# A graph-attention layer: the node stage's loads in another order, and one pair's gathers in other tiles

## The chip, the core and the metric

The kernel runs on one core of a Trainium2 chip. Its time is the device time of one execution in microseconds (us); the median of three runs is given, and a profile of one further execution. The core has a matrix engine (PE, with its weight loads shown apart as PEld), a vector engine (DVE), an activation engine (ACT), GpSimd (POOL) and SyncE (SP). SP computes nothing here: it issues DMAs, in the order of the program. POOL issues the indirect DMAs that gather rows by a list of indices. "SPq" in a row is an instruction of SP's queue.

## What is computed

12,500 nodes with 128 channels, 400,000 edges sorted by their target `dst`, with random sources `src`. Cut to what matters:

```python
h = relu(layernorm(x))                                   # 12500 x 128
t_src, t_dst = h @ w_src, h @ w_dst
m = t_src[src] + b_src + t_dst[dst]                      # 400000 x 128
m = m * edge_weight * radial_mlp(edge_attr_32)
m = m @ w_sep + b_sep                                    # 8 heads of 16 + 16
score = einsum(smooth_leaky_relu(m[:, :, :16]), alpha_dot)
att = segment_softmax(score, dst)
out = x + segment_sum(m[:, :, 16:] * att, dst) @ w_proj + b_proj
```

## The kernel before

**Node stage** (lines 196 to 670). The nodes lie in 98 tiles of 128, worked on in 25 groups of four. Pass 1 (the loop at line 622, `i` from 0 to 24) normalizes a group (ACT and DVE, `norm`), turns it on PE (`turn`, with the maximum with 0 on DVE at line 341), multiplies it by `w_src` (`products(i, 0)`), copies the product out of PSUM on ACT (line 356, into one of six buffers `ms0`) and stores it to the table `t_src` in DRAM by a DMA of SP's queue (line 364). Pass 2 (the loop at line 652, `i` from 0 to 27) does the second product with `w_dst`, and stores two groups at a time to `t_dst` (four buffers `ms1`). Its groups also carry jobs out of the dictionary `extra`, and the raw rows of the first five edge pairs: POOL has gathered those from `x` during pass 1 (40 indirect DMAs, line 378), and pass 2 normalizes and turns them.

A check runs beside pass 1. The sorted targets are loaded into `cur` by four DMAs (`load_targets`, 32 partitions each, line 238) and three for the borders (`load_borders`, lines 243 and 248); `sections` copies each section's first and last target to `ends` on DVE (line 254), `falls` looks for a target below the one before it (line 430), `fits` sums that up and compares single targets (`lim`, read by `load_limits`) with thresholds. The result `bad` chooses, at line 1878, between the windowed edge stage and a general one. `ends` goes to DRAM and back, spread over all partitions (`ends_store`, `ends_load`), for `spans` and `places`. `marks` writes which neighbours differ (`same`). `weights_list` is a list of 36 loads: 15 weights, 14 blocks of weights, four of edge attributes (`load_e`), then `load_d(0)`, `load_w(0)` and `load_w(1)`, whose data lie in early buffers 11, 10 and 12 (see below).

At most eight DMAs of SP's and ACT's queues are out at a time: each takes one of eight semaphores in turn, and SP waits until the DMA that had it eight issues ago has landed.

**Edge stage** (`step(k)`, line 1597, 391 pairs of 1,024 edges). Step `k` does, for pair `k`: transposes of the gathered source rows into PSUM (`sources`, line 1130; for the first five pairs a product of the raw rows, line 1126), the term of the targets (`message`, line 1142, from target rows `md` that `load_md` fetched from `t_dst` and `split_md` split in two on ACT and DVE, lines 1058 and 1060), the radial network one to three steps ahead (`mlp1`, `mlp2`, `mlp3`), scores for pair `k - 1`, and values and sums for pair `k - 12`. `gather(k + 2, f)` issues eight indirect DMAs for a pair on POOL, one for 128 edges (line 1070). POOL has nothing else to do in this stage, so it runs as far ahead as buffers allow: pairs 5 to 12 go to `early`, buffers shared with the messages; pairs from 13 (`AHEAD`) on to six tiles `gs0` and six `gs1` (`GSB` = 6) that are used in turn, so that pair 19's DMAs wait until PE has transposed pair 13. The tiles `xs` and `gu`, one each, belong to work on finished nodes, the first of which is done at pair 40.

Early buffer 10 holds the edge weights of pair 0 until `radial(0)` (line 1119) has read them; pair 10's gather waits for that, and pair 12's for `radial(1)`.

Of the kernel before, what the change touches and what calls it, by code (L numbers as in the profile page):

```python
# [11 lines left out]
F32 = mybir.dt.float32  # L12
# [43 lines left out]
def gnn_kernel(ctx: ExitStack, tc: tile.TileContext, a: dict, out: bass.AP):  # L56
# [34 lines left out]
    def done(k):  # L91

        return 2 * (k - LAG - 2) + 2
# [102 lines left out]
    with tc.tile_pool(name="node1", bufs=1) as n1, tc.tile_pool(name="node", bufs=2) as np_, \  # L196
# [65 lines left out]

        def load_limits():

            with nc.allow_non_contiguous_dma(reason="single targets"):
                u = 0
                for k, d, n in UNIT_RUNS:
                    at = dst[done(k) * SEC:done(k) * SEC + 1]
                    nc.sync.dma_start(out=lim[:, u:u + n], in_=bass.AP(at.tensor, at.offset, [[1, 1], [2 * d * SEC, n]]))
                    u += n  # L270
                nc.sync.dma_start(out=lim[:, UNITS:UNITS + 1], in_=dst[EARLY * SEC:EARLY * SEC + 1].unsqueeze(0))
                nc.sync.dma_start(out=lim[:, UNITS + 1:UNITS + 2],
                                  in_=dst[(NS - 1) * SEC:(NS - 1) * SEC + 1].unsqueeze(0))
                nc.sync.dma_start(out=lim[:, UNITS + 2:UNITS + 3], in_=dst[2 * D * SEC:2 * D * SEC + 1].unsqueeze(0))

        def weights_list():

# [335 lines left out]
        stats(*quads[3])  # L613
        stats(*quads[4])
        roots(quads[3][0], quads[4][1])
        nc.sync.dma_start(out=w_dst, in_=a["w_dst"])
        load_limits()
        load_borders()
        more = iter(weights_list())
        for _ in range(6):  # L620
            next(more)()
        for i in range(Q):
            if i + 1 < Q:
                turn(i + 1)
            if i == 0:
                scales(quads[3][0], quads[4][1])
            if i + 3 < Q:
                norm(i + 3)
            products(i, 0)
            for j in (5, 6) if i == 0 else (i + 6,):  # L630
                if j < Q:
                    stats(*quads[j])
            j = i - i % 2 + 5
            if j < Q:
                (scales if i % 2 else roots)(quads[j][0], quads[min(j + 1, Q - 1)][1])
            if 2 <= i < 6:
                load_targets(i - 2)
            if i == 8:
                sections()
            if i > 8:  # L640
                next(more)()
            if 9 <= i < 13:
                falls(i - 9)
            if i == 14:
                fits()
            if i == 15:
                ends_store()
            if i == 18:
                ends_load()
        extra = {0: lambda: marks(0), 1: lambda: marks(1), 3: lambda: marks(2), 5: lambda: marks(3),  # L650
                 7: lambda: (spans(), places()), 10: cuts, 12: direct_ids, 14: spreads}
        for i in range(2 * RQ + 8):
            if i < Q:
                products(i, 1)
            if i % 2 == 0 and 0 <= i // 2 - 4 < RQ:
                raw_turn(i // 2 - 4)
            q = i // 2 - 1
            if i % 4 == 2 and q < RQ:
                raw_roots(q, q + 2)
            if i % 4 == 3 and q < RQ:  # L660
                raw_scales(q, q + 2)
            if i % 2 == 0 and 0 <= q - 1 < RQ:
                raw_norm(q - 1)
            if i in extra:
                extra[i]()
            for load in (next(more, None), next(more, None)):
                if load:
                    load()
            if i == 2 * RQ:
                nc.scalar.activation(silu, eps[0:1, :], AF.Silu)  # L670

    chunks = [(t, min(CH, TPI - t)) for t in range(0, TPI, CH)]

# [309 lines left out]
    def windows():  # L983
# [7 lines left out]
        with tc.tile_pool(name="ps", bufs=1, space=PSUM) as pp, \  # L991
# [70 lines left out]
            def gather(k, f):  # L1062
                if k < RAW:
                    return
                gs = early[k][:, f * SEC:(f + 1) * SEC].rearrange("p (t c) -> p t c", c=C) if k < AHEAD else \
                    lp.tile([P, TS, C], F32, name=f"gs{f}", bufs=GSB)
                u = k // 16
                idx = prep[u]
                t0 = (k % 16 * 2 + f) * TS
                sent = [nc.gpsimd.indirect_dma_start(  # L1070
                    out=gs[:, t, :], out_offset=None, in_=t_src[:, :],
                    in_offset=bass.IndirectOffsetOnAxis(ap=idx[:, t0 + t:t0 + t + 1], axis=0))
                    for t in range(tiles(k, f))]
                gath[k, f] = gs, sent
# [495 lines left out]
            def has(k):  # L1570
                return 0 <= k < NP
# [25 lines left out]
            def step(k):  # L1597
# [353 lines left out]
```

## Time and profile before

| | us |
|---|---|
| median of three runs | 4060.97 (4060.41 to 4062.98) |
| the profiled execution | 4063.28 |
| its span, first to last instruction | 4061.5 |
| PE busy (95% of the span) | 3860.1 |
| DVE busy (76%) | 3104.7 |
| POOL busy (75%) | 3033.9 |
| ACT busy (46%) | 1881.2 |

A row of the page's groups gives line, engine and operation, the tiles written and read, the count, the busy time and the mean of one in ns, and the idle time of the engine just before these instructions with what ended it. In a timeline a row is the start, the duration, the instruction, and in brackets the idle time of its engine before it and what ended that. Rows of the same kind that follow each other are merged, with their count. The chain of waits that ended last breaks off after a few instructions here and shows nothing.

### The profile page before, as it was taken

What the parts mean: (1) busy time and instruction counts of PE and PEld (TensorE: products, weight loads), DVE (VectorE), ACT (ScalarE), POOL (GpSimd) and SP (SyncE); (2) the same over time, 40 slices, a digit from 0 to 9 for tenths busy, and PEclk for the clock granted to TensorE, in tenths of its full rate; (3) what the DMA queues carried; (4) which work ended last, traced back from release to release, by engine and by line L of the source; (5) the groups of instructions that cost most, each with busy time, mean ns of one, the idle gap of its engine ahead of it and who ended that gap; (6) DMA issues with size and microseconds to landing.
All of it is one profiled execution on the core that took longest, in us unless ns stands there. A gap on an engine that the chain in (4) does not pass through costs nothing. (4 is left out here: it accounts for less than half of the span.)

```text
span 4061.5 us, 84578 instructions
## 1 busy us (share of the span) xinstructions
PE 3860.1 (95%) x27826; PEld 2345.3 (58%) x27826; DVE 3104.7 (76%) x5579; ACT 1881.2 (46%) x3825; POOL 3033.9 (75%) x3193
## 2 busy tenths in 40 slices
PE   6899999999999999999999999999999999999997
PEld 6355655555655555555555555555555555555555
DVE  7577777777777777777777777777777777777876
ACT  6554444444454444444444444444444444444441
POOL 5777777777777777777777777777777777777775
PEclk8999999999999999999999999999999999999998
DMA  7777777777777777776777777777777777777772
GB/s 237 215 176 197 195 198 195 192 185 192 201 180 191 195 184 178 191 188 179 186 186 193 184 185 195 190 180 190 199 191 183 195 189 195 181 201 198 195 183 59
DMA packets 534922, 764.24 MB, mean 188 GB/s; under 512 B 123966, under 2 KB 336862, under 8 KB 534363
## 3 DMA queue, kind: packets, MB, share of 16 engines
q1 hardware_dynamic: 431003, 549.87, 46.8%
q0 software_dynamic: 101888, 207.34, 24.4%
q8 instruction: 226, 3.70, 0.4%
q14 instruction: 221, 1.81, 0.2%
q10 hardware_dynamic: 1584, 1.51, 0.1%
HBM read 633.31 MB, written 126.68 MB: 187 GB/s over the span
## 5 line engine op out<-in xcount | busy, mean ns | idle before, releaser
L1070 POOL DMA_INDIRECT gs<-t_src,idx x3021 | 2876.1, 952 | 928.0 <-issue 772.2
L1155 ACT ACTIVATE sl<-pa,c_b_a 128x512 f32<-128x512 f32 x781 | 537.1, 688 | 1090.1 <-PE pa L1153 1086.3
L1160 DVE SCALAR_TENSOR_TENSOR al<-pa,sl 128x512 f32<-128x512 f32 x781 | 536.8, 687 | 517.1 <-ACT sl L1155 508.4
L1285 PEld LDWEIGHTS V<-c_w_v,mT 128*128 128x128 f32 x6154 | 751.4, 192 | 306.5 <-DVE ob L1302 122.4
L1285 PE MATMUL V<-c_w_v,mT 128*128 128x128 f32 x6154 | 885.2, 287 | 1.9 <-DVE pvx L1287 1.8
L1153 PE MATMUL pa<-mT,c_w_a 128*128 128x512 f32 x1562 | 834.6, 616 | 30.2 <-DVE mT L1147 27.8
L1287 DVE TENSOR_TENSOR pvx<-V,Pem 128x512 f32<-128x512 f32 x770 | 528.3, 686 | 213.9 <-PE V L1285 187.1
L1130 PEld LDWEIGHTS pm<-ident,gs 128*128 128x128 f32 x3021 | 372.7, 141 | 485.7 <-issue 465.1
L1101 ACT ACTIVATE h<-p,b 128x512 f32<-128x512 f32 x391 | 470.0, 1202 | 389.7 <-PE p L1099 379.6
L1119 DVE SCALAR_TENSOR_TENSOR rad<-p,c_fc_b,w_b 128x1024 f32<-128x1024 f32 x389 | 498.3, 1281 | 91.8 <-PE p L1114 71.3
L1130 PE MATMUL pm<-ident,gs 128*128 128x128 f32 x3021 | 457.7, 274 | 64.7 <-DMA gs<-t_src,idx 63.9
L1298 PEld LDWEIGHTS misc<-pvx,oh 128*64 128x64 f32 x6250 | 351.4, 137 | 289.8 <-ACT h L1089 280.6
L1147 DVE SCALAR_TENSOR_TENSOR mT<-pm,c_b_src,rad 128x1024 f32<-128x1024 f32 x391 | 497.7, 1273 | 12.2 <-PE pm L1142 11.7
L1298 PE MATMUL misc<-pvx,oh 128*64 128x136 f32 x6250 | 451.3, 286 | 0.1
L1114 PE MATMUL p<-h,w3b 64*128 64x512 f32 x1564 | 403.1, 592 | 0.0
L1086 PE MATMUL m<-eT,w1b 64*128 64x256 f32 x782 | 274.2, 431 | 18.5 <-ACT qT L1393 14.8
L1142 PE MATMUL pm<-ohT,m 64*128 64x512 f32 x1564 | 287.5, 445 | 0.0
L1153 PEld LDWEIGHTS pa<-mT,c_w_a 128*128 128x128 f32 x1562 | 236.4, 191 | 79.7 <-DVE mT L1147 49.3
L1186 ACT ACTIVATE Sp<-m,b_s 128x512 f32<-128x512 f32 x192 | 131.8, 686 | 309.5 <-PE m L1170 307.3
L1086 PE MATMUL misc<-eT,w1b 64*128 64x256 f32 x782 | 274.2, 431 | 0.0
L1089 ACT ACTIVATE h<-misc,b 128x256 f32<-128x256 f32 x391 | 185.5, 474 | 182.7 <-PE misc L1086 171.3
L1099 PE MATMUL p<-h,w2b 64*64 64x256 f32 x3128 | 261.9, 405 | 0.0
(234 smaller groups left out, 3544.6 us busy)
## 6 DMA issues: line engine op xcount, KB each, us to landing
w_b<-in_edge_weight SPq DMA_DIRECT2D x388, 512.0 KB
d_b<-in_dst SPq DMA_DIRECT2D x388, 256.0 KB
sc_d<-Sp SPq DMA_DIRECT2D x192, 256.0 KB
e_t<-in_edge_attr SPq DMA_DIRECT2D x381, 128.0 KB
gs<-t_src,idx POOLq DMA_INDIRECT x3021
win<-ob SPq DMA_DIRECT2D x390, 68.0 KB
agg<-ob SPq DMA_DIRECT2D x760, 33.5 KB
md<-t_dst SPq DMA_DIRECT2D x782, 32.0 KB
```

Of the source, the lines that this page charges most:

```text
L1070: sent = [nc.gpsimd.indirect_dma_start(out=gs[:, t, :], out_offset=None, in_=t_src[:, :], in_offset=bass.IndirectOffsetOnAxis(ap=idx[:, t0 ...
L1086: nc.tensor.matmul(p1[f], w1b[s, :], eTs[k][s, :], start=True, stop=True)
L1101: nc.scalar.activation(h2s[k].rearrange("x (h i b) -> x h b i", h=2, b=2 * TS), p2[:, :, 0:2 * T].rearrange("x h (b i) -> x h b i", b=2 * TS),
L1119: nc.vector.scalar_tensor_tensor(rad[:, 0:n], p3.rearrange("c f e -> c (f e)")[:, 0:n], b3, w_g[k][:, 0:n], op0=ALU.add, op1=ALU.mult)
L1130: turned = [nc.tensor.matmul(pm[:, t * T:(t + 1) * T], gs[:, t, :], ident, start=(t == 0), stop=False, is_transpose=True, skip_group_check ...
L1147: nc.vector.scalar_tensor_tensor(mTs[k][:, 0:n], pms.rearrange("c f e -> c (f e)")[:, 0:n], b_n, rad[:, 0:n], op0=ALU.add, op1=ALU.mult)
L1153: nc.tensor.matmul(pa[:, 0:n], w_a, mTs[k][:, f * SEC:f * SEC + n], start=True, stop=True)
L1155: nc.scalar.activation(sl[:, 0:n], pa[:, 0:n], AF.Silu, bias=b_a, scale=1.0)
L1160: nc.vector.scalar_tensor_tensor(al, pa, 0.25, sl, op0=ALU.mult, op1=ALU.add)
L1285: nc.tensor.matmul(V[:, t, :], mTs[c][:, o:o + T], w_v, start=True, stop=True)
L1287: nc.vector.tensor_mul(pvx[c][:, f, 0:n, 0:C].rearrange("p t (h k) -> p t h k", h=H), V[:, 0:n, :].rearrange("p t (h k) -> p t h k", h=H), ...
L1298: nc.tensor.matmul(acc[f * W:(f + 1) * W, :], ohs[c][:, f * TS + t, :], pvx[c][:, f, t, :], start=(t == 0), stop=(t == n - 1), skip_group_ ...
```

## The change

In pass 1, SP's queue no longer issues the load of `w_dst`, the limits, the borders and six weights ahead of the stores to `t_src`. The borders are loaded at group 6, the limits at groups 7 to 11 (one run of them at a time), `w_dst` at group 12, the list of weights from group 13 on. The check moves later: `sections` from group 8 to 11, `falls` from 9-12 to 12-15, `fits` from 14 to 17, `ends_store` from 15 to 16, `ends_load` from 18 to 19. In pass 2 one load a group is issued, not two, which makes it 24 loads in groups 0 to 23; `marks` moves from groups 0, 1, 3, 5 to 15, 16, 18, 20. In the edge stage, pair 0's `split_md` moves from step -1 to step 0, behind `radial(0)`, and pair 19 is gathered into the tiles `xs` and `gu`.

```diff
         def load_limits():
-            with nc.allow_non_contiguous_dma(reason="single targets"):
-                u = 0
-                for k, d, n in UNIT_RUNS:
-                    at = dst[done(k) * SEC:done(k) * SEC + 1]
+            u = 0
+            for k, d, n in UNIT_RUNS:
+                at = dst[done(k) * SEC:done(k) * SEC + 1]
+                with nc.allow_non_contiguous_dma(reason="single targets"):
                     nc.sync.dma_start(out=lim[:, u:u + n], in_=bass.AP(at.tensor, at.offset, [[1, 1], [2 * d * SEC, n]]))
-                    u += n
...
+                u += n
+                yield
+            for s_ in (EARLY, NS - 1, 2 * D):
+                nc.sync.dma_start(out=lim[:, u:u + 1], in_=dst[s_ * SEC:s_ * SEC + 1].unsqueeze(0))
+                u += 1
+            yield
...
-        nc.sync.dma_start(out=w_dst, in_=a["w_dst"])
-        load_limits()
-        load_borders()
         more = iter(weights_list())
-        for _ in range(6):
-            next(more)()
+        limits = load_limits()
         for i in range(Q):
...
             if 2 <= i < 6:
                 load_targets(i - 2)
-            if i == 8:
+            if i == 6:
+                load_borders()
+            if 7 <= i < 12:
+                next(limits)
+            if i == 11:
                 sections()
-            if i > 8:
+            if i == 12:
+                nc.sync.dma_start(out=w_dst, in_=a["w_dst"])
+            if i > 12:
                 next(more)()
-            if 9 <= i < 13:
-                falls(i - 9)
-            if i == 14:
+            if 12 <= i < 16:
+                falls(i - 12)
+            if i == 17:
                 fits()
-            if i == 15:
+            if i == 16:
                 ends_store()
-            if i == 18:
+            if i == 19:
                 ends_load()
-        extra = {0: lambda: marks(0), 1: lambda: marks(1), 3: lambda: marks(2), 5: lambda: marks(3),
-                 7: lambda: (spans(), places()), 10: cuts, 12: direct_ids, 14: spreads}
+        extra = {7: lambda: (spans(), places()), 10: cuts, 12: direct_ids, 14: spreads,
+                 15: lambda: marks(0), 16: lambda: marks(1), 18: lambda: marks(2), 20: lambda: marks(3)}
         for i in range(2 * RQ + 8):
...
-            for load in (next(more, None), next(more, None)):
-                if load:
-                    load()
+            load = next(more, None)
+            if load:
+                load()
...
             def gather(k, f):
...
-                gs = early[k][:, f * SEC:(f + 1) * SEC].rearrange("p (t c) -> p t c", c=C) if k < AHEAD else \
-                    lp.tile([P, TS, C], F32, name=f"gs{f}", bufs=GSB)
+                if k < AHEAD:
+                    gs = early[k][:, f * SEC:(f + 1) * SEC].rearrange("p (t c) -> p t c", c=C)
+                elif k == AHEAD + GSB:
+                    gs = sp.tile([P, TS, (C, ROW)[f]], F32, name=("xs", "gu")[f], bufs=1)[:, :, 0:C]
+                else:
+                    gs = lp.tile([P, TS, C], F32, name=f"gs{f}", bufs=GSB)
...
-                if has(k + 1):
+                if has(k + 1) and k >= 0:
                     split_md(k + 1, 0)
...
-                if has(k + 1):
+                if has(k + 1) and k >= 0:
                     split_md(k + 1, 1)
...
                 if has(k):
                     radial(k)
+                if k == 0:
+                    for i in range(2):
+                        split_md(0, i)
```

How this moves instructions is seen at three places. First SP's queue in pass 1, before (`x_all` is the input, `lim` the limits, `cur` the targets, `c_...` weights, `ms0` products):

```order
L243 DMA cur_136<-in_dst 1x2176
L248 DMA cur_136<-in_dst 111x1 x2
L295 DMA c_dot_142<-in_dot 128x1
L295 DMA c_heads_143<-in_heads 128x128
L295 DMA c_b_a_151<-in_b_a 128x1
L295 DMA c_w_proj_153<-in_w_proj 128x128
L295 DMA c_b_proj_154<-in_b_proj 128x128
L295 DMA c_b_v_155<-in_b_v 128x1
L364 DMA t_src_60<-ms0_305 128x512
L364 DMA t_src_60<-ms0_329 128x512
L364 DMA t_src_60<-ms0_352 128x512
L238 DMA cur_136<-in_dst 32x3584
```

The same queue in the change, from the store of group 1 on (group 0's stands just ahead of it, right behind the last load of `x`):

```order
L365 DMA t_src_60<-ms0_312 128x512
L365 DMA t_src_60<-ms0_335 128x512
L238 DMA cur_136<-in_dst 32x3584
L365 DMA t_src_60<-ms0_358 128x512
L238 DMA cur_136<-in_dst 32x3584
L365 DMA t_src_60<-ms0_382 128x512
L238 DMA cur_136<-in_dst 32x3584
L365 DMA t_src_60<-ms0_405 128x512
L238 DMA cur_136<-in_dst 15x3584
L365 DMA t_src_60<-ms0_429 128x512
L243 DMA cur_136<-in_dst 1x2176
L248 DMA cur_136<-in_dst 111x1 x2
```

The borders stood ahead of the first store, and now stand behind the seventh; seventeen DMAs are gone from ahead of the first store. Next DVE around the copy of `sections` (`ends<-cur`), before, then in the change (`pt` is a group's turned tile; its number tells the groups apart):

```order
L341 TENSOR_SCALAR x_all_113<-pt_475 128x512
L330 TENSOR_SCALAR h_481<-x_all_113,rstd_160,shift_161 128x128
L308 BN_STATS mv_159<-x_all_113 128x6 x2
L254 COPY ends_139<-cur_136 112x7 x2
L341 TENSOR_SCALAR x_all_113<-pt_500 128x512
```

```order
L342 TENSOR_SCALAR x_all_113<-pt_532 128x512
L331 TENSOR_SCALAR h_538<-x_all_113,rstd_160,shift_161 128x128
L309 BN_STATS mv_159<-x_all_113 128x6 x2
L318 RECIPROCAL rstd_160<-rstd_160 128x8
L319 SCALAR_TENSOR_TENSOR shift_161<-mv_159,rstd_160 128x8
L254 COPY ends_139<-cur_136 112x7 x2
L342 TENSOR_SCALAR x_all_113<-pt_561 128x512
```

Before, the copy stood between the maxima of groups 9 and 10; now it stands between those of groups 12 and 13. Last POOL at pairs 18 to 20 (a row is four indirect DMAs; `gs0` and `gs1` are the two halves' tiles), before, then in the change:

```order
L1070 DMA gs0_2624<-t_src_60,idx_1685 128x128 x4
L1070 DMA gs1_2669<-t_src_60,idx_1685 128x128 x4
L1070 DMA gs0_2727<-t_src_60,idx_1685 128x128 x4
L1070 DMA gs1_2781<-t_src_60,idx_1685 128x128 x4
L1070 DMA gs0_2836<-t_src_60,idx_1685 128x128 x4
```

```order
L1078 DMA gs0_2624<-t_src_60,idx_1685 128x128 x4
L1078 DMA gs1_2669<-t_src_60,idx_1685 128x128 x4
L1078 DMA xs_2727<-t_src_60,idx_1685 128x128 x4
L1078 DMA gu_2781<-t_src_60,idx_1685 128x128 x4
L1078 DMA gs0_2836<-t_src_60,idx_1685 128x128 x4
```

The gathers stand in the same places; pair 19's have other tiles, and so pairs 20 to 25 take the turn one later: pair 20 needs pair 13's tiles, pair 21 those of pair 14, and from pair 26 on it is again six pairs back.

More of the change, by code (lines that the diff above doesn't have):

```diff
@@ L665, in gnn_kernel @@
                 extra[i]()
-            for load in (next(more, None), next(more, None)):
-                if load:
-                    load()
+            load = next(more, None)
+            if load:
+                load()
             if i == 2 * RQ:
                 nc.scalar.activation(silu, eps[0:1, :], AF.Silu)
+        assert next(more, None) is None and next(limits, None) is None
     chunks = [(t, min(CH, TPI - t)) for t in range(0, TPI, CH)]
```

4 lines of the change are left out of this document (removed).

## The prediction

> **What bounds the kernel now.** I read the page first, then POOL's row of groups, then POOL's timeline from the first gather out of `t_src` to the last, and only then the node stage. The page shows PE busy for 95% of the span, which would make PE the bound. Its groups say otherwise:
>
> ```profile
> L1070 POOL DMA_INDIRECT gs<-t_src,idx x3021 | 2876.1, 952 | 928.0 <-issue 772.2
> L1130 PE MATMUL pm<-ident,gs 128*128 128x128 f32 x3021 | 457.7, 274 | 64.7 <-DMA gs<-t_src,idx 63.9
> ```
>
> PE waits 63.9 us for gathered rows, so it is not always the last. POOL is called idle before its gathers for 928 us, but most of that is 0.30 us before each of them, and nobody ends it ("issue"): it is part of a gather's price. The timeline of POOL shows where it really waited, and the row for the long stretch behind shows that it never did again:
>
> ```profile
> 60.00 0.94 POOL L378 DMA_INDIRECT mT<-in_x,idx  x1 [0.31 <-issue]
> 82.60 2.39 POOL L1070 DMA_INDIRECT mT<-t_src,idx  x1 [21.65 <-DVE shiftr L394]
> ...
> 134.12 0.95 POOL L1070 DMA_INDIRECT mT<-t_src,idx  x1 [0.30 <-issue]
> ...
> 230.41 0.94 POOL L1070 DMA_INDIRECT gs<-t_src,idx  x1 [6.25 <-PE pm L1130]
> 236.36 0.94 POOL L1070 DMA_INDIRECT gs<-t_src,idx  x1 [1.25 <-PE pm L1130]
> 241.35 0.94 POOL L1070 DMA_INDIRECT gs<-t_src,idx  x1 [0.30 <-issue]
> ...
> 301.40 0.94 POOL L1070 DMA_INDIRECT gs<-t_src,idx  x1 [0.30 <-issue]
> 3967.16 0.94 POOL L1070 DMA_INDIRECT gs<-t_src,idx  x1 [0.30 <-PE misc L1298]
> ```
>
> ```profile
> L1070 POOL DMA_INDIRECT gs<-t_src,idx x2965 | 2823.0, 952 | 904.1 <-issue 756.1 <-DMA gs<-t_src,idx 46.6 <-PE pm L1130 22.5
> POOL gs L1070 <- PE pm L1130: 22.5, 74, 0.3
> ```
>
> The second fence is the row of groups, and a row of waits, for the stretch from pair 20 on. 2823.0 + 904.1 = 3727.1 us, and 241.35 + 3727.1 = 3968.4, the end of the last gather: POOL runs through without a pause, and its longest wait for PE is 0.3, the usual gap. That is 1.257 us a gather and 10.06 a pair. So the end is made of four pieces: when POOL may begin on `t_src` (82.60), its stalls at pair 19 (at 230.41 and 236.36), 1.257 us a gather, and a tail of 4061.5 - 3968.1 = 93.4 us behind the last one. The change touches the first two alone. PE, with 63.9 us of waits in hand, only has to release buffers in time.
>
> What holds 82.60? POOL's raw gathers end at 60.94; it waits for all of `t_src`. (DVE L394 is merely the last semaphore that moved.) The node stage's rows:
>
> ```profile
> 15.46 0.56 ACT L356 COPY ms<-pm 128x512 f32<-128x512 f32 x1
> 22.40 0.23 SPq L272 DMA_DIRECT2D lim<-in_dst  x1
> 27.64 1.37 SPq L364 DMA_DIRECT2D t_src<-ms  x3
> 30.55 0.59 ACT L356 COPY ms<-pm 128x512 f32<-128x512 f32 x1 [3.83 <-DMA t_src<-ms]
> 12.89 0.67 DVE L341 TENSOR_SCALAR x_all<-pt 128x512 f32<-128x512 f32 x1
> 25.30 0.69 DVE L341 TENSOR_SCALAR x_all<-pt 128x512 f32<-128x512 f32 x1
> 44.47 0.25 DVE L254 COPY ends<-cur 112x7 int32<-112x7 int32 x2 [11.16 <-DMA t_src<-ms]
> 72.78 0.38 DVE L341 TENSOR_SCALAR x_all<-pt 128x212 f32<-128x212 f32 x1 [0.34 <-PE pt L339]
> 78.92 0.36 SPq L366 DMA_DIRECT2D t_src<-ms  x1
> ```
>
> ```profile
> SPq L272 <- DMA x_all<-in_x: 1.7, 1, 1.7
> 22.00:29.00 7.00, 5.78 (x41) 4.39 (x39) 4.54 (x13) 4.72 (x13) 5.33 (x6) 1.00 0.41 90
> 29.00:45.00 16.00, 4.02 (x16) 3.21 (x16) 2.43 (x9) 6.38 (x16) 11.88 (x13) 0.53 1.00 283
> ```
>
> The first product is copied at 16.02, but SP only stores it at 27.64: it walks through limits, borders and weights. The load that L272 waited for, one of the last of `x`, landed at 22.4. Between 22 and 29 the DMA engines are 41% busy (90 GB/s); from 29 to 45 they are full (283 GB/s), since stores and target loads now come together. ACT runs out of its six buffers (3.83 us), and DVE waits 11.16 us at `sections` for the targets.
>
> **The change part by part.**
>
> *Pair 19's tiles.* Nothing uses `xs` and `gu` until pair 40, so both waits fall to the usual gap: 6.25 - 0.30 = 5.95 and 1.25 - 0.30 = 0.95, together **6.9 us**. The gathers write the same bytes. What is late next is pair 26, for which see below.
>
> *Stores first, in pass 1.* Stores go out as the copies end, from 16.02, behind the loads of `x`, whose bytes keep the engines until 22.4. Before, from the first store to the copy of `ends` it took 44.47 - 27.64 = 16.8 us for six stores and four target loads. The same list now moves from 22.4: 39.2. The start-up of the first store (in the 16.8) falls away, and one more store (256 KB, 0.9 us at 283 GB/s) and three small border loads come in; I call these even. So the targets are there 5.3 us sooner. The copy also stands three groups later. A group costs DVE (25.30 - 12.89) / 7 = 1.77 where nothing waits; less behind it, where the check's instructions stand between; I take 1.6, so 4.8 us of the groups that had to be done after the wait are now done ahead of it. DVE gets there at about 25.30 + 4 x 1.77 + 1.6 = 34, and still waits some 5 us. The end of pass 1's last maximum moves from 72.78 by 5.3 + 4.8 = 10.1. Behind it, 82.60 - 72.78 = 9.8 us pass until POOL starts; `ends_load` now stands one group nearer the end, with five DMAs on SP ahead of the last stores, 0.3 us later by my count of SP's issues. Net **9.8 us** earlier, so POOL starts at 72.8. The limits and the weights, still on SP, come one a group, each in a gap between two stores. Bounds: if the targets land no sooner than 44.47, only 4.8 - 0.3 = 4.5 is left; if DVE does not wait at all, it is 5.2 more, 15.0.
>
> The Trainium skill ("DMA: Bandwidth & Descriptors", Queues, rings and completion order) says that each DMA engine takes the descriptors of one ring in order. By that rule a target load cannot pass the stores issued ahead of it, and the sum is the one above; if it could, the wait would go and the total would be 21.9. The trace agrees with the rule: DVE's copy was released as a store to `t_src` landed.
>
> *Pass 2.* PE's side, for what it has to release:
>
> ```profile
> 106.29 2.08 PE L350 MATMUL pm<-w_dst,x_all 128*128 128x128 f32 x8 [6.47 <-ACT ms L356]
> 105.65 0.59 ACT L356 COPY ms<-pm 128x512 f32<-128x512 f32 x1 [9.66 <-DMA t_dst<-ms]
> 87.51 1.15 SPq L582 DMA_DIRECT2D same<-gt  x2
> 91.44 0.85 SPq L173 DMA_DIRECT2D e_t<-in_edge_attr  x1
> 94.85 25.03 SPq L364 DMA_DIRECT2D t_dst<-ms  x10
> 123.25 5.16 SPq L1052 DMA_DIRECT2D md<-t_dst  x6
> 126.30 0.30 ACT L1058 CAST m<-md 128x128 fp32r<-128x128 f32 x1 [3.66 <-DMA md<-t_dst]
> 130.82 1.28 DVE L1119 SCALAR_TENSOR_TENSOR rad<-p,c_fc_b,mT 128x1024 f32<-128x1024 f32 x1 [1.58 <-PE p L1114]
> 85.00:97.00 12.00, 8.98 (x57) 8.46 (x58) 8.51 (x45) 6.32 (x15) 8.96 (x10) 0.72 0.96 285
> ```
>
> The four writes of `same`, the edge attributes, `load_d` and the two `load_w` stand ahead of ten stores; ACT waits 9.66 us for a buffer and PE 6.47 for ACT. In the change these loads (0.5 + 0.8 + 0.5 + 1.0 = 2.8 MB) come from group 17 on. The stall of 6.47 should go. But the bytes are then moved beside the last stores (1.6 MB): 4.4 MB at 285 GB/s are 15.4 us, where eight groups at some 1.3 take 10.4, so the last store lands 5.0 later than it could. `split_md` at step 0 takes ACT's wait of 3.66 out of step -1, where PE's first products of the radial network stood behind it; it now lies beside `mlp1` to `mlp3`. PE's first steps so come 9.8 + 6.5 - 5.0 + 3.7 = **15.0 us** earlier, between 9.8 (only pass 1) and 20 (no backlog). `marks` on DVE moves to groups 15 to 20, beside ACT's work, which is the longer there; uncovered it would cost its own 4 us on PE's side only. `w_dst` is needed in pass 2 first, `bad` long before POOL's branch.
>
> *Pair 26.* It reuses pair 20's tiles:
>
> ```profile
> 296.75 0.60 PE L1130 MATMUL pm<-ident,gs 128*128 128x128 f32 x4
> ```
>
> PE freed them at 297.35, 4.05 us before POOL's 301.40. POOL comes 9.8 + 6.9 = 16.7 us earlier, so PE must come 12.65 earlier; it comes 15.0. Pairs 20 to 25 have the tile of seven pairs back, and are safe.
>
> **Sum.** 9.8 + 6.9 = 16.7 us. Of the profiled execution's 4063.28 (its span 4061.5) that leaves 4046.6; that execution lies 2.3 above the median, from which I count: 4060.97 - 16.7 = **4044.3**.
>
> **Rivals.**
>
> 1. *POOL runs into PE at pair 26.* If PE's start moves by less than 12.65, POOL waits for the rest: at the lower bound of 9.8, by 2.85, and the gain is 13.9, 4047.1. For it speak the loads that now crowd the end of pass 2; against it the 6.47 and 3.66 us of waits in the rows above, either of which is enough.
> 2. *The wait at `sections` is moved, not shortened.* If targets and borders behind the stores land as much later as the copy was moved, POOL starts at 82.6 as before, and only pair 19's 6.9 stays: 4054.1. For it speaks that the engines are full from 29 to 45; against it the 41% between 22 and 29.
> 3. *The weights of pair 0 come too late, and it gets slower.* `load_w(0)` is now issued at group 22, and pair 10's gather must wait until `radial(0)` has read it. Before, that ended at 132.1 and POOL came at 134.12. Should pass 2 not get shorter and pay for its late bytes in full, 2.8 MB at 285 GB/s or 9.8 us, and for the 3.9 us that SP spends on the writes of `same` (87.51 to 91.44), `radial(0)` ends at 145.8. POOL is then held 11.7, less the 6.9 of pair 19: 4.8 slower, 4065.8. It decides from a `radial(0)` that ends behind 141.0. Against it: pass 2 would have to lose 8.9 us and all of pass 1's gain.
>
> **How the numbers follow.** 0.66 for the forecast (its own range 4039.1 to 4049.6, by the bounds 15.0 and 4.5), 0.20 for the first rival, 0.09 for the second, 0.05 for the third. About 0.2%, 8.1 us, can be told from no change here. The forecast and the first rival lie beyond it: 0.86 faster. The second lies within it, and I give 0.02 of the third to it: 0.11. Slower stays 0.03. The range goes from 4037, the upper bound's 4039.1 less the 2 us by which runs differ, to 4055, which takes in the second rival.
>
> **What would show it.** Right: POOL's first gather from `t_src` near 72.8; DVE's wait at `sections` near 5 us, ending near 39; no wait of ACT for `t_src<-ms`; pairs 18, 19 and 20 without a gap above 0.3; nothing at pair 26; the span shorter by what POOL's 241.35 moved. Wrong: a first gather after 78, a wait of POOL for PE at pair 26 or for DVE at pair 10, or POOL's spacing above 1.257 us, which would put the gain in doubt whatever the node stage does.

## The result and the profile after

| | before | after |
|---|---|---|
| median (lowest to highest), us | 4061.97 (4060.41 to 4065.26), 6 runs | 4047.51 (4044.66 to 4053.24), 6 runs |
| ratio, 95% interval | | 0.9964, 0.9951 to 0.9977 |
| the profiled execution, its span | 4063.28, 4061.5 | 4053.24, 4051.5 |

The change is 14.5 us faster, 4061.97 - 4047.51. The profiled execution of the changed kernel is the longest of its six, and its span shows a gain of 10.0 only; where the steps stand is read from it all the same. Lines of the node stage are now one higher, those of the edge stage eight: the gather is line 1078, the transposes 1138. The timeline of the changed kernel first, POOL, PE, DVE, SP and ACT one behind another:

```profile
72.18 0.94 POOL L1078 DMA_INDIRECT mT<-t_src,idx  x1 [11.42 <-DMA c_fc_b<-in_fc_b]
...
215.46 0.97 POOL L1078 DMA_INDIRECT xs<-t_src,idx  x1 [0.30 <-issue]
225.46 0.94 POOL L1078 DMA_INDIRECT gs<-t_src,idx  x1 [0.30 <-PE misc L1306]
...
290.19 0.94 POOL L1078 DMA_INDIRECT gs<-t_src,idx  x1 [4.88 <-PE pm L1138]
122.01 0.51 PE L1150 MATMUL pm<-ohT,m 64*128 64x512 f32 x2 [1.35 <-ACT m L1062]
...
289.32 0.60 PE L1138 MATMUL pm<-ident,gs 128*128 128x128 f32 x4
38.27 0.25 DVE L254 COPY ends<-cur 112x7 int32<-112x7 int32 x2 [3.11 <-DMA cur<-in_dst]
60.72 0.38 DVE L342 TENSOR_SCALAR x_all<-pt 128x212 f32<-128x212 f32 x1 [0.31 <-PE pt L340]
104.99 1.26 SPq L367 DMA_DIRECT2D t_dst<-ms  x1
114.90 5.10 SPq L1056 DMA_DIRECT2D md<-t_dst  x6
74.23 0.58 ACT L357 COPY ms<-pm 128x512 f32<-128x512 f32 x1 [3.14 <-DMA t_dst<-ms]
...
114.60 0.34 ACTq L173 DMA_DIRECT2D e_t<-in_edge_attr  x1
114.98 0.47 ACT L1097 ACTIVATE h<-misc,b 128x256 f32<-128x256 f32 x1 [9.01 <-DMA t_dst<-ms]
120.74 0.30 ACT L1062 CAST m<-md 128x128 fp32r<-128x128 f32 x1 [3.84 <-DMA md<-t_dst]
```

The start is where it was forecast: the first gather from `t_src` at 72.18 (72.8 forecast), DVE's wait 3.11, ending at 38.27 (some 5, ending at 39). Pair 19 (at 215.46) and pair 20 (at 225.46) have the usual gap of 0.30. But at pair 26, which takes pair 20's tiles, POOL waits 4.88 us, until PE's transposes of pair 20, begun at 289.32, are done: this is the first rival. PE is 296.75 - 289.32 = 7.4 us earlier, not 15.0.

The rows of the page's groups for the same two lines, and then the windows (PE, PEld, DVE, ACT and POOL busy, clock, DMA share, GB/s):

```profile
L1078 POOL DMA_INDIRECT gs<-t_src,idx x3013 | 2871.6, 953 | 923.0 <-issue 759.6
L1138 PE MATMUL pm<-ident,gs 128*128 128x128 f32 x3013 | 456.0, 274 | 73.6 <-DMA gs<-t_src,idx 73.0
```

```profile
85.00:97.00 12.00, 10.89 (x91) 9.86 (x89) 11.79 (x31) 8.48 (x21) 9.87 (x8) 1.00 0.65 216
97.00:104.00 7.00, 1.95 (x7) 1.11 (x8) 2.35 (x6) 3.98 (x10) 5.17 (x7) 0.69 0.95 293
104.00:115.00 11.00, 4.92 (x18) 1.34 (x15) 1.07 (x2) 0.86 (x3) 8.26 (x10) 0.66 0.87 267
```

PE now waits 73.0 us for gathered rows (63.9 before): it is still not the bound in the long run. The windows show the end of pass 2: the DMA engines are 65% busy between 85 and 97, then 95% and 87%, while ACT is busy 0.86 of 11 us. The last store of `t_dst` is issued at 104.99, and SP, which loads `md` from that table, comes to it only at 114.90. Before, these were 119.97 and 123.25; the first is this row of the timeline before:

```profile
119.97 0.77 SPq L366 DMA_DIRECT2D t_dst<-ms  x1
```

### The profile page after: what moved, and what is told of

Its sections match the earlier page's. It is cut to its first block, busy times and chain, and to the rows that moved or that the text cites. A ratio compares the mean times of both kernels' runs of the same rounds, so it can differ in the third digit from the quotient of the medians.

```text
span 4051.5 us, 84580 instructions
## 1 busy us (share of the span) xinstructions
PE 3856.9 (95%) x27826; PEld 2342.0 (58%) x27826; DVE 3104.1 (77%) x5579; ACT 1879.9 (46%) x3825; POOL 3038.5 (75%) x3193
## 5 line engine op out<-in xcount | busy, mean ns | idle before, releaser
L1277 DVE TENSOR_TENSOR oh<-lane,misc 128x504 f32<-128x504 f32 x391 | 262.1, 670 | 0.0
```

## The experiments

All kernels together, read from their timelines (us). "md" is SP's first load of `md`; "PE 20" the start of PE's transposes of pair 20; "26" the start of pair 26's gathers. (Line numbers differ by a few between these kernels.) The medians stand beside those of the kernel before in the same session: 4064.43 (17 runs, 4058.95 to 4073.82) for the four rows from "pair 19 alone" on, 4065.57 (18, 4060.02 to 4075.94) for the next four, 4064.23 (12, 4056.93 to 4071.84) for the last four; the changed kernel's own is in the first table.

| kernel | first gather | last store | md | PE 20 | PE 20 - md | wait at 26 | 26 | median, lowest to highest | ratio to before, 95% |
|---|---|---|---|---|---|---|---|---|---|
| before | 82.60 | 119.97 | 123.25 | 296.75 | 173.5 | 0.30 | 301.40 | above | |
| changed | 72.18 | 104.99 | 114.90 | 289.32 | 174.4 | 4.88 | 290.19 | 4047.5 (4044.7-4053.2) | 0.9964 (0.9951-0.9977) |
| pair 19 alone | 83.57 | 120.88 | 124.27 | 298.50 | 174.2 | 4.17 | 299.37 | 4061.3 (4054.6-4069.9) | 0.9993 (0.9985-1.0002) |
| loads alone | 71.99 | 105.94 | 114.53 | 289.36 | 174.8 | 0.30 | 294.00 | 4052.0 (4048.4-4054.3) | 0.9965 (0.9952-0.9978) |
| spare tiles | 72.07 | 104.84 | 114.18 | 288.80 | 174.6 | 0.30 | 285.09 | 4046.3 (4043.8-4050.1) | 0.9954 (0.9942-0.9967) |
| large loads first | 70.23 | 102.96 | 106.03 | 279.50 | 173.5 | 0.30 | 282.89 | 4048.8 (4043.4-4052.9) | 0.9960 (0.9947-0.9973) |
| split back | 71.68 | 103.64 | 111.61 | 285.20 | 173.6 | 1.68 | 286.07 | 4051.6 (4046.0-4053.9) | 0.9962 (0.9948-0.9976) |
| `sections` at 8 | 76.13 | 107.14 | 116.28 | 290.51 | 174.2 | 2.81 | 291.38 | 4058.3 (4050.5-4061.4) | 0.9977 (0.9967-0.9987) |
| marks early | 69.31 | 98.67 | 107.13 | 281.44 | 174.3 | 2.40 | 282.31 | 4043.1 (4041.4-4046.9) | 0.9944 (0.9927-0.9960) |
| small loads first | 77.37 | 110.56 | 118.77 | 293.96 | 175.2 | 4.04 | 294.83 | 4057.3 (4052.5-4061.0) | 0.9976 (0.9966-0.9987) |
| changed, again | 71.53 | 104.53 | 113.97 | 288.69 | 174.7 | 4.18 | 289.56 | 4049.7 (4046.0-4051.5) | 0.9969 (0.9957-0.9981) |
| loads of `e_t` on SP | 71.25 | 104.70 | 113.20 | 289.06 | 175.9 | 5.30 | 289.93 | 4050.1 (4047.2-4053.4) | 0.9967 (0.9956-0.9978) |
| three edits | 71.95 | 100.27 | 103.22 | 279.23 | 176.0 | 0.30 | 282.62 | 4043.2 (4040.1-4045.8) | 0.9954 (0.9941-0.9968) |
| spare tiles, marks early | 69.72 | 98.75 | 107.84 | 282.54 | 174.7 | 0.30 | 280.91 | 4041.5 (4039.4-4042.3) | 0.9948 (0.9935-0.9962) |

Two things hold in every row. PE comes to pair 20 between 173.5 and 176.0 us after the first `md` load, though that load moves by 21 us. And where POOL waits at pair 26, its gathers start 0.87 us after PE's transposes of pair 20. What follows pair 26 is less constant: in single executions it took from 3753.4 (pair 19 alone, span 4052.8) to 3765.9 us (`sections` at 8, span 4057.3), in the profiled executions before and after 3760.1 and 3761.3. Of this the rest of POOL's gathers takes 3663.0 to 3670.6, and the work behind the last of them 88.9 to 97.5. So a mechanism is read from the columns of the profile, and a gain of time from medians.

**Pair 19 alone.** The kernel before, with only

```diff
-                gs = early[k][...] if k < AHEAD else lp.tile(..., name=f"gs{f}", bufs=GSB)
+                if k < AHEAD:
+                    gs = early[k][...]
+                elif k == AHEAD + GSB:
+                    gs = sp.tile([P, TS, (C, ROW)[f]], F32, name=("xs", "gu")[f], bufs=1)[:, :, 0:C]
+                else:
+                    gs = lp.tile([P, TS, C], F32, name=f"gs{f}", bufs=GSB)
```

> The kernel before with one part of the change alone: pair 19's gathers go into the two tiles of the units' stage. Theory: POOL's two waits at pair 19 (5.95 and 0.95 us) go, so POOL would reach pair 26 at 301.40 - 6.9 = 294.5, but PE, whose start is not touched, frees pair 20's tiles only at about 297.65. A new wait of about 3.1 us stands at pair 26, and the gain against the kernel before is about 3.8 us. Rival (the term as the prediction has it, each part by itself): nothing stands at pair 26, and the gain is 6.9 us.

Its timeline, POOL and then PE:

```profile
299.37 0.94 POOL L1074 DMA_INDIRECT gs<-t_src,idx  x1 [4.17 <-PE pm L1134]
298.50 0.60 PE L1134 MATMUL pm<-ident,gs 128*128 128x128 f32 x4
```

The waits at pair 19 are gone and one of 4.17 stands at pair 26. The 6.9 us are taken out at one place, and 3.9 of them (4.17 - 0.30) come back seven pairs later. The ratio's interval takes in 1: alone, this part cannot be told from no change.

**The reordered loads alone.** The changed kernel with the old lines for `gs` (the diff above, reversed).

> The changed kernel with the old tiles for pair 19, that is, the reordered loads alone. Theory: POOL now comes to pair 19 at about 215.5, and PE frees pair 13's tiles at about 223.0, so the wait at pair 19 grows from 5.95 to about 7.5, with about 1 behind it; pair 26 then starts near 293.7 with no wait, about 3.5 us behind the changed kernel's 290.2, and the time is 3.5 us above the changed kernel's, that is, about 10.5 to 11 below the kernel before. Rival (the parts add up): the 6.9 us of pair 19 come back in full, and the time is 6.9 above the changed kernel's, about 7.6 below the kernel before.

Its timeline at pair 19:

```profile
223.02 0.94 POOL L1074 DMA_INDIRECT gs<-t_src,idx  x1 [8.52 <-PE pm L1134]
...
228.97 0.94 POOL L1074 DMA_INDIRECT gs<-t_src,idx  x1 [1.26 <-PE pm L1134]
```

POOL waits here until 223.02, and pair 26 starts at 294.00, both as the theory has them: 3.8 us behind the changed kernel, not 6.9. The two parts do not add up; POOL takes at each pair the later of its own time and PE's. In time this kernel is 12.4 us below the kernel before of its session (4064.43 - 4051.99), where 10.5 to 11 were expected and the changed kernel has 14.5; the intervals of the two ratios overlap, so the medians alone do not tell the two apart.

**Spare tiles for three pairs.**

```diff
-                elif k == AHEAD + GSB:
+                elif k in (AHEAD + GSB, AHEAD + 2 * GSB + 1, AHEAD + 3 * GSB + 2):
```

> The changed kernel with the units' two tiles used for pairs 26 and 33 as well, so that each pair from 20 to 39 has the tiles of seven pairs back instead of six. Theory: the 4.88 us at pair 26 are a wait for PE's transposes of pair 20 and nothing else; they go, pair 26 starts at about 285.6, no wait stands at 33 or 40, and the time falls by about 4.6 to 4.9 us against the changed kernel, to about 4042.7, with less spread, since PE's start no longer sets the end. Rival: POOL meets PE again a few pairs later (at 27 to 34 or at 40), and less than 2 us of it is kept.

```profile
285.09 0.94 POOL L1078 DMA_INDIRECT xs<-t_src,idx  x1 [0.30 <-PE pm L1150]
...
295.07 0.95 POOL L1078 DMA_INDIRECT gs<-t_src,idx  x1 [0.30 <-PE pm L1150]
```

The timeline of this kernel has pair 26 at 285.09 and pair 27 at 295.07 without a wait, and none stands at 33 or 40. PE is where it was (288.80), so the 4.88 were a wait for pair 20's tiles and nothing else. The time is 18.1 us below the kernel before of its session (4064.43 - 4046.33), against 14.5 in the changed kernel's own; 4.6 to 4.9 more were expected, 3.6 more came, and the two ratios' intervals overlap. The wait is shown to go; what that is worth in time is not.

**The large loads of pass 2 ahead of the small.** In `weights_list`:

```diff
-            return [... for t, ap in pairs] + [load_e ... range(4)] + [load_d(0), load_w(0), load_w(1)]
+            small = [... for t, ap in pairs]
+            return small[:7] + [load_e ... range(4)] + [load_d(0), load_w(0), load_w(1)] + small[7:]
```

> The changed kernel with the loads of pass 2 in another order: the four loads of edge attributes and the loads of targets and edge weights for the first pairs (2.0 MB) come ahead of the remaining small weights, so that their bytes move while the DMA engines are less busy, and not beside the last stores of the node table. Theory: PE's start is late because these bytes hold the last store up (it was issued at 104.99 and landed near 114.5); the store lands 4 to 6 us sooner, ACT's 9.0 us behind it shrink by as much, pair 20's transposes come 4 to 5 us earlier (near 285), the wait at pair 26 falls below 1 us, and the time is 4 to 5 us below the changed kernel's. Rival 1: PE's start is set by PE's own steps or by DVE, and the wait at pair 26 stays within 1 us of 4.88. Rival 2: the bulk now delays the stores of the first table or POOL's first gathers, and what pair 26 gains is lost there.

```profile
102.96 0.38 SPq L368 DMA_DIRECT2D t_dst<-ms  x1
106.03 5.12 SPq L1057 DMA_DIRECT2D md<-t_dst  x6
...
279.50 0.60 PE L1139 MATMUL pm<-ident,gs 128*128 128x128 f32 x4
```

In its timeline the last store goes out only 2.0 us earlier than in the changed kernel, as much as its first gather, but `md` follows it after 3.1 us instead of 9.9, PE comes to pair 20 at 279.50, and the wait at pair 26 is gone. The table shows the same in the whole series: where the large loads come early (before, pair 19 alone, this one, the three edits) the gap from the last store to `md` is 2.95 to 3.4 us, in all others 8.0 to 9.9. So it is those loads that hold the end of pass 2 up. In time it is not shown: the profiled execution is the fastest of five, and the median of 4048.8 is no better than the changed kernel's 4049.7 of the other session.

**Pair 0's split back in step -1.**

```diff
-                if has(k + 1) and k >= 0:
+                if has(k + 1):
                     split_md(k + 1, 0)
...
-                if k == 0:
-                    for i in range(2):
-                        split_md(0, i)
```

> The changed kernel with the split of pair 0's windows back in step -1, ahead of the first products of the radial network, as it was in the kernel before. Theory (the move was worth its 3.7 us, as the prediction's term says): ACT's cast again waits for the window loads until about 120.7 ahead of what PE needs, the message of pair 0 comes about 4 us later (near 127.7), pair 20's transposes near 293, and the wait at pair 26 grows from 4.88 to about 8.7; pair 26 starts near 294. Rival: in the changed kernel ACT waits 3.84 us for the same load after all, now at step 0, so the move brought PE nothing, and pair 20's transposes stay within 1 us of 289.3.

```profile
103.64 0.76 SPq L367 DMA_DIRECT2D t_dst<-ms  x1
...
111.61 5.10 SPq L1056 DMA_DIRECT2D md<-t_dst  x6
285.20 0.60 PE L1138 MATMUL pm<-ident,gs 128*128 128x128 f32 x4
```

Neither came out as written: PE was 4.1 us earlier. The timeline shows where. `md` was loaded 3.3 us earlier, ahead of any split: up to that load every engine runs the same instructions in the same order in both kernels. `sections` at 8, with the split where the change put it, has the same 40 us from first gather to `md` (39.9 here, 40.2 there; 42.7 in the changed kernel, and what makes the difference was not found). From `md` to pair 20 it is 173.6 against 174.4. The move was worth nothing that can be seen, 0.8 us the wrong way at most, and the median (4051.6) says no better of undoing it.

**`sections` back at group 8, and SP's small loads back at the front.** Two kernels, one for each half of the 9.8 us forecast for pass 1:

```diff
-            if i == 11:
+            if i == 8:
                 sections()
```

```diff
         limits = load_limits()
+        nc.sync.dma_start(out=w_dst, in_=a["w_dst"])
+        for _ in range(5):
+            next(limits)
+        load_borders()
+        for _ in range(6):
+            next(more)()
         for i in range(Q):
...
-            if i == 6:
-                load_borders()
-            if 7 <= i < 12:
-                next(limits)
...
-            if i == 12:
-                nc.sync.dma_start(out=w_dst, in_=a["w_dst"])
-            if i > 12:
+            if i > 18:
                 next(more)()
```

> The changed kernel with the copy of the sections' ends back at group 8 of pass 1; the stores first and all else stay. Theory (the prediction's 4.8 us for the three groups that now run ahead of the wait): the targets and borders still land near 38.2, DVE comes to the copy some 5 us sooner and waits about 8 instead of 3.1, and POOL's first gather from the node table moves from 72.2 to about 77. Rival: the end of pass 1 is set by the stores' transfers and not by DVE; the first gather stays within 1 us of 72.2.

> The changed kernel with SP's small loads (the destination weights, limits, borders and six weights) back ahead of pass 1's stores and target loads; the copy of the sections' ends stays at group 11, and pass 2 is as in the changed kernel. Theory (the prediction's 5.3 us for the order of SP's queue): SP comes to its first store near 27.6 instead of 16, the targets land near 43.6, DVE waits about 8.5 at the copy instead of 3.1, and POOL's first gather moves from 72.2 to about 77.5. Rival: the position of the copy alone made the gain, the targets land where they did, and the first gather stays within 1 us of 72.2.

The timeline of the first, DVE and POOL:

```profile
36.89 0.25 DVE L254 COPY ends<-cur 112x7 int32<-112x7 int32 x2 [7.52 <-DMA cur<-in_dst]
76.13 1.02 POOL L1078 DMA_INDIRECT mT<-t_src,idx  x1 [14.95 <-DMA c_fc_b<-in_fc_b]
```

and of the second:

```profile
44.67 0.41 DVE L254 COPY ends<-cur 112x7 int32<-112x7 int32 x2 [3.50 <-DMA t_src<-ms]
77.37 1.49 POOL L1078 DMA_INDIRECT mT<-t_src,idx  x1 [16.46 <-DMA c_fc_b<-in_fc_b]
```

Both theories hold for POOL's start. With the copy at group 8 the targets land no later (36.89), DVE waits 7.52 instead of 3.11, and POOL starts 4.0 us later (4.8 in the prediction). With the small loads in front the copy comes at 44.67, 6.4 later, and POOL 5.2 later (5.3 in the prediction). DVE's wait is only 3.50 there, not the 8.5 expected: it comes to the copy later, since ACT now waits for its six buffers, whose stores begin at 26.99. The row of waits of that kernel between 14 and 46 (in all, times, longest) has it, where the changed kernel waits once, 1.5 us:

```profile
ACT ms L357 <- DMA t_src<-ms: 7.7, 3, 3.2
```

In time both lose more than that. They are 7.2 and 8.2 us below the kernel before, against 14.5, although `sections` at 8 starts pair 26 only 1.2 later than the changed kernel (291.38 against 290.19). In its trace 3765.9 us lie behind pair 26, against 3761.3 and 3756.6 in the two of the changed kernel, and nothing in the edit says why.

**The marks' comparisons early.**

```diff
-                 15: lambda: marks(0), 16: lambda: marks(1), 18: lambda: marks(2), 20: lambda: marks(3)}
+                 0: lambda: marks(0), 1: lambda: marks(1), 3: lambda: marks(2), 5: lambda: marks(3)}
```

> The changed kernel with the four comparisons that make the marks back at groups 0, 1, 3 and 5 of pass 2, and so the writes of the marks (0.78 MB) earlier on SP's queue. Theory: four gathers between 88 and 97 took 1.49, 1.55, 1.62 and 1.87 us because each began while DVE ran one of these comparisons (1.09 us) and went on with the next instruction without a pause; with the comparisons ahead of POOL's first gather these gathers take 0.94 to 1.04, and pair 8 starts at about 102.4 instead of 105.0. The writes leave the end of pass 2, so PE's transposes of pair 20 come up to 3 us sooner; the wait at pair 26 stays at 4 to 5, and the time falls by about 3 us. Rival: the gathers are slow because the DMA engines are full; they stay at 1.5 to 1.9, and pair 8 stays at 105.0.

What it was aimed at, in the timeline of the changed kernel, POOL and then DVE:

```profile
88.52 1.49 POOL L1078 DMA_INDIRECT mT<-t_src,idx  x1 [0.30 <-issue]
90.32 1.55 POOL L1078 DMA_INDIRECT mT<-t_src,idx  x1 [0.30 <-issue]
...
93.42 1.62 POOL L1078 DMA_INDIRECT mT<-t_src,idx  x1 [0.30 <-issue]
95.35 1.87 POOL L1078 DMA_INDIRECT mT<-t_src,idx  x1 [0.30 <-issue]
88.11 1.09 DVE L579 TENSOR_TENSOR gt<-cur 112x896 bf16<-112x896 int32 x1
...
89.97 1.09 DVE L579 TENSOR_TENSOR gt<-cur 112x896 bf16<-112x896 int32 x1
...
93.14 1.09 DVE L579 TENSOR_TENSOR gt<-cur 112x896 bf16<-112x896 int32 x1
...
95.32 1.09 DVE L579 TENSOR_TENSOR gt<-cur 112x896 bf16<-112x896 int32 x1
```

and the same stretch with the marks early:

```profile
88.35 0.99 POOL L1078 DMA_INDIRECT mT<-t_src,idx  x1 [0.30 <-issue]
...
95.89 0.95 POOL L1078 DMA_INDIRECT mT<-t_src,idx  x1 [0.30 <-issue]
```

with the window's row:

```profile
85.00:97.00 12.00, 8.76 (x63) 7.19 (x63) 6.99 (x19) 11.27 (x27) 9.09 (x10) 0.90 0.97 333
```

The theory holds: the slow gathers are gone, though the DMA engines are fuller there (97% against 65%), which rules the rival out. PE gained more than expected: the last store left 6.3 us earlier and PE came 7.9 earlier. Of this 2.9 is a first gather at 69.31, for which the order of instructions gives no reason (see the end). The wait at pair 26 is 2.40, where 4 to 5 were expected. In time this kernel is 22.5 us below the kernel before of its session (4065.57 - 4043.12), against 14.5; it has four runs, and the intervals of the two ratios overlap a little.

**Loads of edge attributes on SP instead of ACT.**

```diff
-                    load_e(k + 6, nc.scalar)
+                    load_e(k + 6, nc.sync)
```

> The changed kernel with the loads of edge attributes for pairs 4 to 12 issued by SP instead of ACT. Theory: ACT's wait of 9.01 us ahead of the first products' activations is not for the table itself; ACT stands at the issue of such a load, whose semaphore is still held by an earlier transfer of the crowded queue. On SP the load waits just as long, but ACT goes on at once: the 9.01 and PE's 5.69 at 115.87 fall below 3, pair 20's transposes come 1 to 4 us earlier, and the wait at pair 26 shrinks as much. Rival: ACT needs what lands at 114.5 itself; both waits stay within 1 us of where they were.

```profile
118.28 0.30 ACT L1062 CAST m<-md 128x128 fp32r<-128x128 f32 x1 [9.64 <-DMA md<-t_dst]
119.55 0.80 PE L1150 MATMUL pm<-ohT,m 64*128 64x512 f32 x2 [7.67 <-ACT m L1062]
```

Half a hit. The 9.01 us at line 1097 are gone, so ACT did not need what landed there; it stood at the issue of a DMA, the load of `e_t` at 114.60, which in the trace uses the semaphore of the store issued at 104.27. But the timeline has a wait of 9.64 in its place, at the next instruction that does need the table, and PE waits 7.67 for that. PE comes to pair 20 at 289.06, 0.3 earlier. The wait had moved, not shrunk; `md` was the bound behind it.

**The changed kernel again, and two that are meant to be better.**

> The changed kernel once more, unaltered, beside the three that follow, so that they stand against it on one chip. Theory: POOL's first gather lies within 2 us of 72.2, the wait at pair 26 is again there and is between 2 and 7 us, since it is the difference of two moments (PE's transposes of pair 20 and POOL's arrival) that both move with the transfers at the end of pass 2; four gathers between 88 and 97 again take 1.3 to 1.9 us. Rival: the wait at pair 26 was a chance of the one profile and is not there.

> Three edits together: the units' tiles for pairs 19, 26 and 33, the marks' comparisons early in pass 2, and the large loads of pass 2 ahead of the small weights. Theory: the wait at pair 26 (4.9) and the slow gathers beside the comparisons (2.7) both go, and since neither gives back the other's gain the time falls by 7 to 8 us against the changed kernel; POOL runs from its first gather to its last without a wait above 0.4. Rival: the early bytes (2.8 MB, at 285 GB/s some 10 us) now lie beside the last stores of the first table, POOL's first gather comes 3 us or more later, and less than 4 us is kept.

> The same without the reordered large loads: the units' tiles for pairs 19, 26 and 33 and the marks' comparisons early. Theory: with the tiles of seven pairs back PE's start no longer sets anything, so this is within 1.5 us of the version with all three edits, although PE starts later here. Rival: PE's start still reaches the end, and this version is 3 us or more above it.

The wait at pair 26 is there again, 4.18 us, with the slow gathers. The three edits together are 6.6 us below the changed kernel (4049.71 - 4043.15), where 7 to 8 were expected. Spare tiles with early marks take 4041.5: all five runs (to 4042.3) lie below all six of the changed kernel (from 4046.0), by 8.2 us in the medians, on one chip. Adding the reordered large loads does not help (4043.2; 1.6 us above, where 1.5 was allowed), although PE comes 3.3 us earlier: with a tile to spare, PE's start sets nothing. This is the lowest median found, 0.9948 (0.9935 to 0.9962) of the kernel before. The early marks alone stand at 0.9944 (0.9927 to 0.9960), so that the spare tiles add anything to them in time is not shown; in the timelines they take away the wait of 2.40.

## Why the prediction was right, and where not

The direction, the range (4037 to 4055) and the 4047.5 within it came out; 14.5 us were gained and 16.7 forecast. The mechanism of the likeliest case did not hold to the end: the first rival, with 0.20, is what happened, and its 4047.1 is the nearest of the prices. That it is so near is partly luck. The rival was priced at PE's lower bound of 9.8; with the 7.4 that were measured its own sum gives a gain of 16.7 - (12.65 - 7.4) = 11.5. Pair 26 moved by 11.2, and the median by 14.5.

- **POOL is the bound behind pair 20: right.** The spare tiles moved pair 26 by 5.1 us (290.19 to 285.09) with PE unmoved, and PE's earlier start was worth nothing that shows once they were there (three edits against spare tiles with early marks).
- **Stores first and a later copy, 9.8 us: right in sum and in both parts.** The first gather came 10.4 us earlier. The order of SP's queue was worth 5.2 (5.3 forecast), the place of the copy 4.0 (4.8). Each is the difference of two traces, and kernels with the same pass 1 differ by up to 2.9 in their first gather, so the parts are known to some 3 us. The second rival falls with this. One sign did not hold: ACT still waits once for `t_src<-ms`, 1.5 us.
- **Pair 19, 6.9 us: right at its place, not at the end.** The waits went; what it left over in the end was 3.8 (294.00 - 290.19), because POOL met PE at pair 26.
- **PE 15.0 us earlier: wrong, and the step that failed.** 7.4 were measured, below the lower bound of 9.8. By the prediction's terms: pass 1 and the stall in pass 2 (9.8 + 6.5 = 16.3) moved the last store by 15.0 (119.97 to 104.99), nearly as forecast. The backlog, put at 5.0, cost 6.6 (the gap from the last store to `md`, 9.9 against 3.3). The split, put at +3.7, was -0.9 (173.5 us from `md` to pair 20 before, 174.4 after). 14.98 - 6.63 - 0.92 = 7.43. The largest miss is the split: ACT's 3.66 us for `md` were taken for a delay that could be passed by. But PE's next products need the same `md`: the cast waits 3.84 at its new place, and PE 1.35 for the cast (at 122.01). That this is why the move brought nothing is read from these rows; what the runs show is that the 174 us run from `md`, wherever the cast stands. The lower bound was too high because it counted no loss behind pass 1.
- **Pair 26 needs 12.65 us of PE: right.** With 7.4 it waits; the large loads first gave 17.2 (296.75 - 279.50) and it did not.
- **`marks` beside ACT's work, cost on PE's side only: wrong.** The comparisons lengthened four of POOL's gathers by 2.8 us in all (1.49 + 1.55 + 1.62 + 1.87 - 4 x 0.94), at the engine that is the bound. DVE's row of busy time does not show that; POOL's timeline does.
- **Radial weights of pair 0 (third rival): not seen.** No gather of pairs 10 to 12 waited.

From 82.60 to pair 26 the trace accounts for it so: 10.4 at the start, 1.4 because the first gather took 2.39 us before and 0.94 now, 6.9 at pair 19, less 2.8 beside the marks and 4.6 at pair 26 (4.88 - 0.30): 11.3, against 11.2 (301.40 - 290.19). Behind pair 26 POOL's gathers took 3669.3 us against 3666.7 before, 1.258 us a gather, and a spacing above 1.257 was one of the prediction's signs of being wrong. But in the changed kernel's second trace they took 3666.8, with pair 26 at 289.56, so the slower pace does not come with the change. That the medians differ by 14.5 and the profiled spans by 10.0 stays unexplained in detail: the other runs have no trace.

## What to carry to other kernels

Where one engine runs ahead through a ring of buffers, a removed wait is worth the slack that the other engine has at the next turn of the ring, so price the next turn before adding terms; with one more buffer there the wait was gone, and a start of the other engine that came 3.3 us earlier was then worth nothing. When transfers are taken off the front of a stage, ask what is issued last and who loads from it: here PE's start hung on the load that follows the last store, and moving other waits about it (the split, ACT's 9.01 us) gained nothing. And before work is moved to an idle stretch of one engine, look at which other engine's instructions will run beside it.

## What the runs showed of the hardware

- A gather's issue on POOL is held up by some DVE instructions. Each of the four slow gathers ended 0.81 us after the comparison that ran when it began (88.11 + 1.09 = 89.20 and 88.52 + 1.49 = 90.01; the others likewise: 91.06 and 91.87, 94.23 and 95.04, 96.41 and 97.22); the 740 gathers that begin in the changed kernel while DVE is idle take 0.94 in the mean and none above 1.00. The Trainium skill ("SBUF — State Buffer", SBUF: two separate sides) says that DVE and GpSimd share one pair of ports as an exclusive lock, held for the whole instruction, and that a DVE instruction takes it in a two-port performance mode, or with two inputs in SBUF against a GpSimd instruction that reads SBUF. The comparison has two such inputs, the gather reads its indices from SBUF, and the constant 0.81 behind the comparison's end is what a lock would give; the ports themselves show in no run here. The same trace has it in the edge stage: a gather beside `M<-S,M` (line 1229, two inputs in SBUF) ends at 431.86, 0.82 behind that instruction, after 1.37. Two tensor inputs are not needed: one beside `ohT<-d_b,tgt` (line 1116, one tensor input and a column of scalars) ends at 154.96, again 0.82 behind, after 1.12; no trace here shows in which mode that instruction runs. Beside `pvx<-V,Pem`, which reads one input from PSUM, 383 gathers begin and none takes above 1.01.
- An engine that issues a DMA can stand still for a transfer it has no use for. ACT waited 9.01 us at an activation that has no use for the store that landed; the load of edge attributes stood ahead of it on ACT's queue, and with that load on SP the wait there was gone.
- Kernels with the same pass 1 did not start POOL at the same time: the targets let DVE go on between 35.67 (large loads first) and 38.84 (loads alone), and the first gather came between 69.31 and 72.18 (ten of these kernels run the same instructions in the same order up to pass 1's last maximum, near 60 us). It may not be mere scatter: in the four that have another order in pass 2 (large loads first, marks early, and the two that join edits) DVE went on between 35.67 and 36.69, in the other six between 37.72 and 38.84, though the orders differ only more than 20 us later. What decides it was not found.
